# One layer's second group of feed-forward down products issued inside the next layer's attention

## The chip, the cores and the metric

The kernel runs on one core of a Trainium2 chip. The core has five engines that each work through their own queue in order: TensorE (PE, matrix products; its weight loads are listed apart as PEld), VectorE (DVE), ScalarE (ACT), GpSimd (POOL) and SyncE (SP), which here only issues DMA transfers. Matrix products go from SBUF into banks of PSUM, and DVE or ACT carry them out again. The metric is the device time of one execution in microseconds (us): 835.17 us, the median of three runs (834.82 to 837.08).

## The reference, cut to what matters

The input `x` has 4 x 256 tokens of 256 features; a small context has 4 x 64 rows of 64 features. Four layers follow each other. Each one adds a gated cross-attention and then a gated feed-forward block, both on the layer-normalised stream:

```
x = x + tanh(g_xattn[n]) * xattn_n(layernorm(x), ctx)
x = x + tanh(g_ffn[n])   * ffn_n(layernorm(x))
```

The change stands where the feed-forward block of layer 1 meets the attention of layer 2. Layer 1's block has ternary weights:

```
w1_q, w2_q = absmean_quant(w1), absmean_quant(w2)
h   = gelu(layernorm(x) @ w1_q.T + b1)      # 256 -> 1024
out = h @ w2_q.T + b2                       # 1024 -> 256, the "down" product
```

Layer 2's attention has 16 heads of 16 features and a causal mask over 64 keys:

```
qp   = layernorm(x) @ Wq.T
k, v = split(ctx @ Wkv_expand.T)
attn = softmax(where(causal, qh @ kh.T / 4, lowest))
out  = (attn @ vh) @ Wout.T
```

Every token is normalised on its own, so the attention of a token needs that token's row of `x` and the context, and no other token's row.

## The kernel before, in words

The stream `x` stays in SBUF as eight tiles of 128 tokens (NT = 8). They form two groups of four tiles (NG = 2, TPG = 4): tiles 0 to 3 are the first group, tiles 4 to 7 the second.

**How the order is made.** The Python code emits instructions in program order. A planner then makes the queue of every engine before anything runs: the place in program order is an instruction's priority, and where the planner expects an engine to wait, it lets a later instruction that is ready go first. Once made, the queues are fixed, and on the chip an engine waits at the head of its queue. Tiles with a common tag share a fixed number of buffers: products of one bank (`mm`, line 107) have four PSUM banks, and the tag `xn` has seven SBUF buffers, shared by normalised tiles, by `y` of the down products and by `ctxTok`.

**Layer 1's feed-forward, `ffn1` (line 1852).** `up(g)` makes the hidden values of a group: products with the ternary weights (line 1888), Gelu on ACT (line 1895), and a split of the fp32 values into three bf16 terms (lines 1814 to 1817), which are kept in the array `big`. `down(g, terms)` makes the four output tiles of a group: 8 x 3 = 24 bf16 products accumulate in one bank (line 1904), DVE adds the bias into `y` (line 1912), and `gated_add` (line 511) adds the gated result to `x[t]` on DVE. `in_turn` orders this as `up(0), up(1), down(0), down(1)`. Then `used("L1_w1")` and `used("L1_w2")` free two weight buffers and so issue the next weight loads on SP (line 231), and `load_experts3(4, 8)` issues eight transfers on SP (line 330) that overwrite the hidden values with expert weights of layer 3.

**Layer 2's attention, `keyed(2, ...)`.** It first makes keys and values from the context in `keys_values(2, ...)`: products at lines 989 and 1004, eight DVE operations that spread the keys (line 996), and eight copies of values that alternate between ACT and DVE (lines 169 and 171). This needs no row of `x`. Then `attention23` runs `queries(0)`: the normalisation of the first group (statistics at lines 430 and 433, a square root on ACT at line 435, a reciprocal at 438, the normalised tiles at 449), transposes on PE (line 461), the query products (line 476), and a scaling on ACT (line 1033). `in_flight` then walks through the eight tiles as a software pipeline. At step `i` it calls the generator `beside` once, then emits `scores(i)` (score products at line 1057, mask products at 1047; a row maximum at 1070 and two subtractions at 1072 on DVE; an exponential on ACT at 1081), the weights of tile `i-1` (a sum at 490 and a reciprocal at 491 on DVE, a multiplication on POOL at 492), and `attend(i-2)` (transposes at 506, ACT copies at 507, products with the values at 1089, an ACT copy at 1098, the output products at 1101), with the `gated_add` of tile `i-3` at line 511. `beside` holds two streams side by side: `queries(1)`, which is the same three-step chain for the second group, and the keys and values of layer 3 (lines 989, 992, 1004, 1011).

So the second group's normalisation follows `down(1)`, which is complete before anything of layer 2 is emitted.

Of the kernel before, what the change touches and what calls it, by code (L numbers as in the profile page):

```python
# [30 lines left out]
F32 = mybir.dt.float32  # L31
# [5 lines left out]
ALU = mybir.AluOpType  # L37
# [60 lines left out]
def tile_flamingo(ctx: ExitStack, tc: tile.TileContext, a: dict, out: bass.AP):  # L98
# [16 lines left out]
    def region(tag, cols, name):  # L115
        return sb.tile([P, cols], F32, tag=tag, name=name, bufs=1)
# [899 lines left out]
    def attention23(layer, gate, beside):  # L1016
        kbd, vbd = kept.pop(layer)
        w = loaded[f"L{layer}"]
        w_q = w[:, :512].rearrange("p (c o) -> p c o", c=2)
        w_o = w[:, 512:1024].rearrange("p (c o) -> p c o", c=2)  # L1020
        qT = []

        def queries(g):

            xn = layernorm(g, layer == 3)
            yield
            xT = transposed(xn)
            yield
            pss = [ps_mm() for _ in range(2)]
            for half, ps in enumerate(pss):  # L1030
                mm2(ps, lambda c: w_q[:, c, half * P : (half + 1) * P], xT)
            for half, ps in enumerate(pss):
                nc.scalar.mul(xT[:, half, :], ps, 0.25)
            qT.append(xT)

        for _ in queries(0):
            pass

        def scores(t):


            g, i = divmod(t, TPG)
            ps = ps_wide()
            masked = t % 2 == 0
            if masked:
                for a in range(2):
                    nc.tensor.matmul(
                        ps[:, a, :].rearrange("p (h l) -> p h l", l=L),
                        ident16,
                        causal16.unsqueeze(1).to_broadcast([P, 8, L]),  # L1050
                        start=True,
                        stop=False,
                    )

            def part(half, a):
                rows = slice(a * L, (a + 1) * L)
                return nc.tensor.matmul(
                    ps[:, a, half * D : (half + 1) * D],
                    qT[g][rows, half, i * P : (i + 1) * P],
                    kbd[rows, half, t // 2].rearrange("p i l -> p (i l)"),  # L1060
                    start=not masked,
                    stop=(half == 1 or not masked),
                )

            side_by_side(lambda half=half, a=a: part(half, a) for half in range(2) for a in range(2))

            e = t4([P, NH, L], "attn")
            src = ps.rearrange("p a (h l) -> p (a h) l", l=L)
            mx = small([P, NH], "mx")
            nc.vector.tensor_reduce(mx, src, AX.X, ALU.max)  # L1070
            for a in range(2):
                nc.vector.tensor_tensor(
                    e.rearrange("p (f a i) l -> p a f i l", f=2, a=2)[:, a],
                    ps[:, a, :].rearrange("p (f i l) -> p f i l", f=2, l=L),
                    mx[:, a * 8 : (a + 1) * 8]
                    .rearrange("p (f i) -> p f i", f=2)
                    .unsqueeze(3)
                    .to_broadcast([P, 2, 4, L]),
                    ALU.subtract,
                )  # L1080
            nc.scalar.activation(e, e, AF.Exp)
            return e

        def attend(t, e):
            aT = transposed_pairs(e)
            ps = ps_mm()
            for pr in range(NP):
                half, r = divmod(pr, 4)
                nc.tensor.matmul(
                    ps[r * 32 : (r + 1) * 32, half * P : (half + 1) * P],  # L1090
                    vbd[:, t // 2, pr].rearrange("p j d -> p (j d)"),
                    aT[:, pr, :],
                    start=True,
                    stop=True,
                    tile_position=(0, r * 32),
                )
            cT = sb.tile([P, 2 * P], F32, tag="xn", name="ctxTok", bufs=AHEAD + 2)
            nc.scalar.copy(cT, ps[:, : 2 * P])
            ps = ps_mm()
            for half in range(2):  # L1100
                nc.tensor.matmul(
                    ps[:, :D], cT[:, half * P : (half + 1) * P], w_o[:, half, :], start=(half == 0), stop=(half == 1)
                )
            return ps

        in_flight(scores, attend, gate, zip_longest(queries(1), beside))
        if layer == 3:
            used("L3")

# [7 lines left out]
    def keyed(layer, gate):  # L1117
        beside = iter(())
        if layer == 2:
            values = region("wqk", 2048, "values")  # L1120
            for _ in keys_values(2, region("weff", 2048, "kbd2"), values[:, :1024]):
                pass
            beside = beside2(keys_values(3, region("wvo", 2048, "kbd3"), values[:, 1024:]))
        attention23(layer, gate, beside)
        for _ in beside:
            pass
# [725 lines left out]
    def ffn1(gate):  # L1852
        b2_1 = sb.tile([P, 512], F32, tag="low", name="b2_1", bufs=1)[:, :D]
        nc.sync.dma_start(out=b2_1, in_=a["L1_b2"].partition_broadcast(P))
        w1 = ternary(1).rearrange("p (c f) -> p c f", c=2)
        w2 = ternary(2).rearrange("p (f o) -> p f o", f=8)
        hidden = big[:, HIDDEN:].bitcast(BF16).rearrange("p (g k f t) -> p g k f t", g=NG, k=3, f=8)

        def inputs(g):

            two = sb.tile([P, 2, 2, TH], BF16, tag="xT", name="xT", bufs=2)
            more = t4([P, 1024], "more")
            third = more[:, :512].bitcast(BF16).rearrange("p (c t) -> p c t", c=2)
            xn = layernorm(g)
            for c in range(2):
                ps = ps_mm()
                for i, n in enumerate(xn):
                    nc.tensor.transpose(ps[:, i * P : (i + 1) * P], n[:, c * P : (c + 1) * P], ident)
                rest = more[:, 512:]
                nc.scalar.copy(two[:, 0, c, :], ps)  # L1870
                nc.vector.tensor_tensor(rest, ps, two[:, 0, c, :], ALU.subtract)
                nc.scalar.copy(two[:, 1, c, :], rest)
                nc.vector.tensor_tensor(third[:, c, :], rest, two[:, 1, c, :], ALU.subtract)
            return two[:, 0], two[:, 1], third

        xT = [inputs(0)]

        def up(g):
            for f2 in range(4):
                if g == 0 and f2 == 1:  # L1880
                    xT.append(inputs(1))
                h = t4([P, 2, TH], "h")
                for j in range(2):
                    f = 2 * f2 + j
                    ps = ps_mm()
                    for k, term in enumerate(xT[g]):
                        for c in range(2):
                            nc.tensor.matmul(
                                ps,
                                w1[:, c, f * P : (f + 1) * P],  # L1890
                                term[:, c, :],
                                start=(k == 0 and c == 0),
                                stop=(k == 2 and c == 1),
                            )
                    nc.scalar.activation(h[:, j, :], ps, AF.Gelu, bias=b1_1[:, f : f + 1])
                three_terms([hidden[:, g, k, 2 * f2 : 2 * f2 + 2, :] for k in range(3)], h, h, f2 % 2 == 1)
            return hidden[:, g]

        def down(g, terms):
            for i in range(TPG):  # L1900
                ps = ps_mm()
                for f in range(8):
                    for k in range(3):
                        nc.tensor.matmul(
                            ps[:, :D],
                            terms[:, k, f, i * P : (i + 1) * P],
                            w2[:, f, :],
                            start=(f == 0 and k == 0),
                            stop=(f == 7 and k == 2),
                        )  # L1910
                y = sb.tile([P, D], F32, tag="xn", name="y", bufs=AHEAD + 2)
                nc.vector.tensor_tensor(y, ps[:, :D], b2_1, ALU.add)
                gated_add(g * TPG + i, y, gate)

        in_turn(NG, up, down)
        used("L1_w1")
        used("L1_w2")
        load_experts3(EARLY3, E3)


    def quantised():
# [239 lines left out]
```

## Time and profile before

| | |
|---|---|
| median of three runs | 835.17 us |
| the profiled execution | 835.11 us, its span 833.3 us |
| down products of both groups (line 1904) | 192 products, from 510.64 to 531.69 us of the span |
| layer 2 until the first row maximum (line 1070) | 531.69 to 545.73 us |
| first to last score products (line 1057) | 544.23 to 573.33 us |
| last `gated_add` of layer 2's attention (line 511) | ends at 592.95 us |
| busy over the span | PE 93%, DVE 60%, ACT 35%, POOL 30% |

Times in the trace count from the start of the span. A line of the profile's list of instructions in order of time reads: start, duration, engine, line, operation, output <- input, and in brackets how long the engine had been idle and what released it. Products on PE overlap and their ends are modelled, so the step from one start to the next tells more than a single product's duration. PEclk is the clock that the throttle granted to PE, as a share of full speed.

### The profile page before, as it was taken

To read this page: it belongs to the slowest core of one execution; us is meant where nothing else is said; L and a number is where in the kernel's file an instruction comes from. 1 tells how busy PE (TensorE), PEld (TensorE's weight loads), DVE (VectorE), ACT (ScalarE), POOL (GpSimd) and SP (SyncE) were. 2 spreads that over 40 slices of the span, in tenths; PEclk is the share of its full clock that TensorE was granted. 3 is DMA by queue.
4 is the path that set the end of the run, shared out by engine and by line. 5 is a ranking of instruction groups with operands and counts; after the bars stand their busy time and mean duration, and the time that the engine had idled before them with its cause. 6 is when DMAs were issued, how large, how long until landed. Compare 5 with 4: busy or idle time off the path is not lost. (4 is left out here: it accounts for less than half of the span.)

```text
span 833.3 us, 12472 instructions
## 1 busy us (share of the span) xinstructions
PE 773.2 (93%) x4492; PEld 518.9 (62%) x4492; DVE 497.5 (60%) x1146; ACT 291.4 (35%) x508; POOL 246.0 (30%) x211
## 2 busy tenths in 40 slices
PE   6999999898999999999999989998588899999994
PEld 4544433687574777676565746655335556999993
DVE  5565454874682555444869559779769663333331
ACT  2121112343312333232633477166454521233320
POOL 1355454322122343321031300024413203344322
PEclk9999999999999999999999999899879999999998
DMA  9510205700121254324900001810000102232211
GB/s 333 200 39 0 59 37 197 270 20 6 30 69 43 73 140 84 65 45 121 365 33 7 1 1 32 313 42 1 26 1 1 45 9 81 56 46 46 28 17 17
DMA packets 32467, 62.44 MB, mean 75 GB/s; under 512 B 5552, under 2 KB 19504, under 8 KB 31696
## 3 DMA queue, kind: packets, MB, share of 16 engines
q1 hardware_dynamic: 25008, 51.91, 18.2%
q0 software_dynamic: 7104, 9.41, 6.9%
q8 instruction: 39, 0.64, 0.3%
q10 hardware_dynamic: 288, 0.26, 0.1%
q14 instruction: 28, 0.23, 0.1%
HBM read 52.81 MB, written 9.27 MB: 74 GB/s over the span
## 5 line engine op out<-in xcount | busy, mean ns | idle before, releaser
L492 POOL TENSOR_TENSOR attn<-attn,sm 128x1024 f32<-128x1024 f32 x32 | 61.1, 1911 | 229.2 <-DVE sm L491 178.9
L476 PE MATMUL wide<-xT,big 128*128 128x512 f32 (+1 forms) x240 | 108.6, 600 | 1.1 <-DVE shared L1661 0.9
L736 DVE TENSOR_TENSOR rope<-wide,big 128x512 f32<-128x512 f32 x96 | 59.6, 683 | 52.0 <-PE wide L476 52.0
L476 PEld LDWEIGHTS wide<-xT,big 128*128 128x128 f32 (+1 forms) x240 | 43.4, 188 | 57.3 <-issue 49.3
L1434 PE MATMUL wide<-blk,still 128*128 128x128 f32 x640 | 74.8, 275 | 0.6 <-DVE blk L1406 0.6
L1434 PEld LDWEIGHTS wide<-blk,still 128*128 128x128 f32 x640 | 73.1, 192 | 0.8 <-issue 0.8
L708 PE MATMUL mm<-vo,attnT 128*128 128x256 f32 x256 | 58.6, 382 | 1.5 <-ACT attnT L507 1.5
L476 PE MATMUL wide<-xT,dense 128*128 128x512 f32 (+1 forms) x120 | 55.1, 598 | 0.0
L708 PEld LDWEIGHTS mm<-vo,attnT 128*128 128x128 f32 x256 | 47.8, 190 | 11.4 <-ACT attnT L507 3.2
L507 ACT COPY attnT<-mm 128x512 f32<-128x512 f32 x64 | 34.3, 586 | 46.2 <-PE mm L506 45.7
L490 DVE TENSOR_REDUCE sm<-attn 128x16 f32<-128x1024 f32 x32 | 38.6, 1208 | 15.2 <-ACT attn L484 13.8
L1396 DVE COPY still<-big 128x1024 f32 x20 | 13.9, 694 | 52.1 <-PE wide L1434 44.5
L1468 POOL DMA_INDIRECT out_dram<-ring,scratch x20 | 31.5, 1577 | 39.5 <-DVE ring L1461 15.8
L1468 POOL DMA_INDIRECT sums<-ring,big x17 | 26.9, 1580 | 48.3 <-ACT ring L1550 18.9
L1452 PE MATMUL mm<-big,hidden 128*128 x160 | 37.8, 380 | 1.4 <-DVE hidden L1445 1.4
L506 PE MATMUL mm<-ident,attn 128*128 128x128 f32 x256 | 33.7, 275 | 5.7 <-POOL attn L492 5.7
L1369 POOL DMA_INDIRECT xs<-xd,scratch x20 | 20.1, 1003 | 62.3 <-PE mm L1403 39.3
L511 DVE SCALAR_TENSOR_TENSOR x<-mm,tg,x 128x256 f32<-128x256 f32 x44 | 20.5, 471 | 29.5 <-PE mm L708 18.2
L506 PEld LDWEIGHTS mm<-ident,attn 128*128 128x128 f32 x256 | 29.1, 141 | 13.3 <-POOL attn L492 8.5
L1444 ACT ACTIVATE hidden<-wide 128x512 f32<-128x512 f32 x20 | 12.0, 598 | 71.2 <-PE wide L1434 66.1
L476 PEld LDWEIGHTS wide<-xT,dense 128*128 128x128 f32 (+1 forms) x120 | 21.5, 185 | 24.4 <-issue 22.1
L790 ACT COPY big<-mm 128x512 f32<-128x512 f32 x16 | 8.6, 589 | 68.0 <-PE mm L778 61.7
(359 smaller groups left out, 1571.7 us busy)
## 6 DMA issues: line engine op xcount, KB each, us to landing
big<-in_L_w_gate_up SPq DMA_DIRECT2D x8, 1024.0 KB, 10.7
big<-in_L_w_down SPq DMA_DIRECT2D x8, 512.0 KB, 10.8
w_L_qk<-in_L_qk SPq DMA_DIRECT2D x4, 896.0 KB, 9.5
big<-in_L_w SPq DMA_DIRECT2D x2, 1480.0 KB, 8.1
big<-in_L_w SPq DMA_DIRECT2D x2, 1110.0 KB, 5.4
big<-in_L_wo SPq DMA_DIRECT2D x1, 2048.0 KB, 15.0
big<-in_L_w SPq DMA_DIRECT2D x2, 1024.0 KB, 5.2
xd<-xn SPq DMA_DIRECT2D x16, 128.0 KB, 1.8
```

Of the source, the lines that this page charges most:

```text
L476: nc.tensor.matmul(ps, w(c), xT[:, c, :], start=(c == 0), stop=(c == 1))
L490: nc.vector.tensor_reduce(sm, e, AX.X, ALU.add)
L492: nc.gpsimd.tensor_tensor(e, e, sm.unsqueeze(2).to_broadcast([P, groups, n]), ALU.mult)
L506: nc.tensor.transpose(ps[:, i * P : (i + 1) * P], ev[:, pr * P : (pr + 1) * P], ident)
L507: nc.scalar.copy(aT[:, half * 4 : half * 4 + 4, :].rearrange("p i t -> p (i t)"), ps)
L511: return nc.vector.scalar_tensor_tensor(x[t], ps, gate, x[t], ALU.mult, ALU.add)
L708: nc.tensor.matmul(ps[:, :D], aT[:, s, :], vo[:, s, :], start=(s == 0), stop=(s == NP - 1))
L736: nc.vector.tensor_tensor(m[:, s, :].rearrange("q (b t) -> q b t", t=S), ps[:, s, :].rearrange("q (b t) -> q b t", t=S), table, ALU.mult,)
L1369: nc.gpsimd.indirect_dma_start(out=xs, out_offset=None, in_=self.xd, in_offset=bass.IndirectOffsetOnAxis(ap=self.gather[:, b : b + 1].bitc ...
L1434: made = nc.tensor.matmul(ps[:, k, f : f + P], w[:, at : at + P], st[:, c * P : (c + 1) * P], start=(c == 0), stop=(c == 1),)
L1452: made = nc.tensor.matmul(ps[:, :D], hT[:, j * P : (j + 1) * P], self.w[:, bass.ds(r + j * D, D)], start=(j == 0), stop=(j == n - 1),)
L1468: nc.gpsimd.indirect_dma_start(out=self.sums[b % len(self.sums)], out_offset=bass.IndirectOffsetOnAxis(ap=self.scatter[:, b : b + 1].bitca ...
```

## The change

`down` now makes a single tile, `down(g, i, terms)`. `ffn1` makes both groups' hidden values and the first group's four down tiles. The second group's four down tiles go into a generator `others`, which is put into `kept` and stops after its first and its third tile. Its first tile is asked for in `keyed` after the keys and values of layer 2 are emitted. The rest is chained in front of `queries(1)`: step 0 of `in_flight` emits its second and third tile ahead of `scores(0)`; step 1 emits the fourth tile, frees `L1_w2`, issues the transfers of the experts' weights, and goes on to the second group's normalisation, ahead of `scores(1)`. The steps of `queries(1)` thereby stand one step later than before (1, 2 and 3 in place of 0, 1 and 2). `used("L1_w1")` stands ahead of the down products. In layer 3 `kept` holds no `others`, and nothing changes there.

```
-        in_flight(scores, attend, gate, zip_longest(queries(1), beside))
+        in_flight(scores, attend, gate, zip_longest(chain(kept.pop("others", ()), queries(1)), beside))
...
             for _ in keys_values(2, region("weff", 2048, "kbd2"), values[:, :1024]):
                 pass
+            next(kept["others"])
             beside = beside2(keys_values(3, region("wvo", 2048, "kbd3"), values[:, 1024:]))
...
-        def down(g, terms):
+        def down(g, i, terms):
+            ps = ps_mm()
+            for f in range(8):
+                for k in range(3):
+                    nc.tensor.matmul(
+                        ps[:, :D],
+                        terms[:, k, f, i * P : (i + 1) * P],
+                        w2[:, f, :],
+                        start=(f == 0 and k == 0),
+                        stop=(f == 7 and k == 2),
+                    )
+            y = sb.tile([P, D], F32, tag="xn", name="y", bufs=AHEAD + 2)
+            nc.vector.tensor_tensor(y, ps[:, :D], b2_1, ALU.add)
+            gated_add(g * TPG + i, y, gate)
+
+        terms = [up(g) for g in range(NG)]
+        used("L1_w1")
+        for i in range(TPG):
+            down(0, i, terms[0])
+
+        def others():
             for i in range(TPG):
...
-        in_turn(NG, up, down)
-        used("L1_w1")
-        used("L1_w2")
-        load_experts3(EARLY3, E3)
+                down(1, i, terms[1])
+                if i in (0, 2):
+                    yield
+            used("L1_w2")
+            load_experts3(EARLY3, E3)
+
+        kept["others"] = others()
```

## The prediction

> **What bounds the kernel now.** I read the page first: its busy shares and its 40 slices.
>
> ```profile
> PE 773.2 (93%) x4492; PEld 518.9 (62%) x4492; DVE 497.5 (60%) x1146; ACT 291.4 (35%) x508; POOL 246.0 (30%) x211
> ...
> PE   6999999898999999999999989998588899999994
> PEclk9999999999999999999999999899879999999998
> DMA  9510205700121254324900001810000102232211
> ```
>
> PE sets the time nearly everywhere, and slice 25 (521 to 542 us) is one of the few with a lowered clock. That is where layer 1 meets layer 2, so I asked for busy time there by stage: first group's down products, second group's, layer 2 up to its first row maximum, its dense part, its tail.
>
> ```profile
> core 0: us, PE busy (x) PEld busy (x) DVE busy (x) ACT busy (x) POOL busy (x), PEclk, DMA share, GB/s
> 510.64:521.17 10.53, 10.53 (x98) 9.44 (x97) 10.46 (x18) 5.80 (x7) 0.00 (x0) 1.00 0.25 66
> 521.17:531.69 10.52, 10.52 (x98) 9.24 (x96) 6.74 (x20) 0.30 (x1) 0.00 (x0) 1.00 0.85 302
> 531.69:545.73 14.04, 12.22 (x38) 6.19 (x38) 8.63 (x26) 3.01 (x8) 0.00 (x0) 0.76 0.82 297
> 545.73:576.08 30.35, 28.86 (x205) 16.89 (x205) 29.26 (x43) 20.05 (x37) 11.69 (x9) 1.00 0.00 1
> 576.08:592.40 16.32, 11.87 (x117) 7.93 (x116) 12.23 (x39) 10.57 (x21) 6.59 (x6) 1.00 0.00 1
> ```
>
> In the third stage PE has 38 products in 14 us at a mean clock of 0.76; no engine is full, so a chain of latencies bounds it. In the fourth PE and DVE are both full (28.86 and 29.26 of 30.35). In the last, four attends follow each other. The list in order of time gives the steps:
>
> ```profile
> 531.69 1.13 PE L989 MATMUL mm<-ctxT,w_L 64*128 64x256 f32 x4
> 536.86 2.29 PE L461 MATMUL mm<-ident,xn 128*128 128x128 f32 x8
> 539.61 4.69 PE L476 MATMUL mm<-xT,w_L 128*128 128x512 f32 x8 [0.46 <-ACT xT L169]
> 545.62 1.10 PE L461 MATMUL mm<-ident,xn 128*128 128x128 f32 x8
> 548.13 3.70 PE L476 MATMUL mm<-xT,w_L 128*128 128x512 f32 x8
> 558.17 1.14 PE L1057 MATMUL wide<-kbd,xT 64*128 64x256 f32 x8
> 587.99 1.04 PE L506 MATMUL mm<-ident,attn 128*128 128x128 f32 x8
> ...
> 545.73 1.23 DVE L1070 TENSOR_REDUCE mx<-wide 128x16 f32<-128x1024 f32 x1 [4.35 <-PE wide L1057]
> ...
> 548.96 1.28 ACT L1081 ACT_TABLE_LOAD   x1
> ```
>
> The reader sees the same transposes and queries twice: with the clock down for the first group (2.29 and 4.69 us), at full clock for the second (1.10 and 3.70). DVE waits 4.35 us for the first scores.
>
> **The change, part by part.** All sums are against the profiled execution: 835.11 us, span 833.3, so 1.8 us lie around the span; it stands 0.06 us below the median.
>
> *Moved on PE:* 96 products. 192 take 531.69 - 510.64 = 21.05 us, 0.110 each: 2.63 per tile, 10.5 for the group. None goes away; the gain can only be idle PE time that they fill. What PE must do in the third stage, at full clock, from start-to-start steps: four L989 in 0.97; eight L1004 at 0.63 a pair (560.30 to 560.93), 2.5; transposes 1.03 (545.62 to 546.64); queries 3.63 (548.13 to 551.76); scores of a tile 1.06 (556.00 to 557.06). Sum 9.2 of 14.04, so 4.8 us can be filled at most.
>
> *The new order:* PE is done with the first group at 521.17. Priority then goes: keys and values, tile 4's down, queries(0), tiles 5 and 6, scores(0). Tile 4 waits for a bank of `mm`, since keys and values ask for six of the four; these come free with DVE's eight L996 (2.74 us), so tile 4 starts near 525.9 and I leave 0.9 us of PE idle. After that a down tile fills every wait of queries(0). But tiles 5 and 6 also stand ahead of scores(0), so PE has to finish three down tiles first: 3.5 + 3 x 2.63 + 1.03 + 3.63 + 1.06 + 0.9 = 18.0 us. The first row maximum comes near 539.3 in place of 545.73, 6.4 earlier.
>
> *What is pushed into the full stage:* on PE, tile 7's down, 2.63: the gain by PE is 6.4 - 2.6 = 3.8. On DVE, what stood ahead of 545.73 and now stands behind: y, gated add and statistics of tile 7 (0.42 + 0.48 + 0.43 + 0.18 = 1.5), about half of tile 6's (0.75), reciprocal and four normalised tiles (0.17 + 1.38). Sum 3.8; the gain by DVE is 6.4 - 3.8 = 2.6. DVE is the later of the two. It is not the last word, since tile 7's weights leave POOL at 583.7 and its attend starts only at 587.99 behind the other attends: 4.3 us of slack for DVE, none for PE's chain of attends. Between 2.6 and 3.8 I take 3.0, nearer to DVE, which has no slack before 576.
>
> *The second group's chain* becomes tight. Tile 7's down ends near 541.8; y, gated add, statistics to 543.5; root with a table load (1.28 + 0.30) to 545.1; reciprocal and four tiles to 546.9; transposes and copy (1.03 + 0.69) to 548.8; queries to 552.5; scaling to 553.2. Before it ended at 553.23 as well, and scores(4) ran only at 558.17. So the cover is 5 us less the gain; about 2 us remain.
>
> *ACT tables:* before, the second group's root (539.45) shared a table with the first group's, and one load (548.96) leads to the exponentials. Now the root probably falls between the first two exponentials: two more loads, 2 x 1.28 = 2.57 us, on an ACT that is busy 20.05 of 30.35. Bounds: nothing, or 2.57 if attends wait on the copies behind them; an exponential needs 1.06, a row maximum and its subtractions on DVE 2.5, so DVE covers most. I charge 0.4. [...]
>
> *Clock:* the loss is 2.29 - 1.10 + 4.69 - 3.70 = 2.2 us and is part of the 4.8; with PE filled it should not appear. The clock was lowered although no idle of PE above 0.73 us is listed in 531 to 536. [...]
>
> *SP and banks:* the sgu load and the transfers of experts 6 and 7 (five DMAs, issued from 530.37 to 533.54) go to about 542; those of experts 4 and 5 need only the first group's terms, and either stay near 520 or go with them. SP's next transfer is at 592.07 and landing takes 11 us at the median, the experts are used after 676: cost nothing. The `w1` release moves nothing, its load went out at 510.83. POOL's queue gets nothing new; its next work is the first tile's weights (553.02), earlier with the tile. An early down tile holds a bank of `mm` for 2.63 us that attends want: between 0 and one such wait, inside the 0.4 and 0.9 above.
>
> Sum: 3.0 - 0.4 = 2.6 us; 835.1 - 2.6 = 832.5. This is just over 0.3% (2.5 us), which is about what a measurement of this kernel can tell from no change.
>
> **The rivals.** *Everything is filled and the tail shortens* (0.13): the planner lets scores(0) go ahead of a down tile, all 4.8 us come out, and up to 1 us of the attends' backlog: 829.3 to 831. For it: the slack of 4.3 us at tile 7. Against: tiles 5 and 6 have the higher priority.
>
> *The gain is eaten* (0.19): fixed queues meet a wait that the planner costed otherwise (an early y add heading DVE while its products are not done, the two table loads ahead of an exponential). Each such wait is 1 to 1.3 us (DVE idled 1.00 before each y add); two or three take the 2.6: 834.5 to 836. For it: both engines are full from 545.73 on, so nothing hides a stall there.
>
> *The second group's chain becomes the bound, slower* (0.22): the chain has nine changes of engine, and every one can stand behind a tile's operation (1.2 us on DVE, 1.06 on ACT, 1.1 on PE). With one and a half in front of each, 9 x 1.6 = 14.4 us, scores(4) comes at 567.6. From there, one tile's latency (some 13 us: before, tile 0 took from 544.23 to 560.4, less table load and the second group's work) and three more at the pitch of L1101 (5.0 us) end at 596 in place of 592.9: 838. It decides once scores(4) comes later than 564.5. Against: these operations have a higher priority than the tiles' after them.
>
> **How the numbers follow.** The likeliest case (0.46) is 832.5, its own range 830.5 to 834.5; it lies on the border, so I give 0.28 of it to faster and 0.18 to within 0.3%. Faster: 0.28 + 0.13, with 0.01 from the eaten gain, 0.42. Same: 0.18 + 0.18 = 0.36. Slower 0.22. The range goes from 829.3 (835.1 - 4.8 - 1.0) to 838.0, the slower rival's price; about 0.15 lies outside, nearly all above.
>
> **What would show it.** Right: L1904 in pieces between L989, L461 and L476 after 521; full clock from 521 to 545; first row maximum near 539; two extra table loads; scores(4) from 553 to 556; attention ended near 590. Wrong: a clock that still falls, a first maximum after 542 (then tile 7 and the second group are too late to win anything), or scores(4) behind 558.

## The result, and the profile after

The changed kernel takes 843.32 us (median of seven runs, 839.01 to 845.98), the kernel before 837.08 us beside it (seven runs, 834.82 to 838.43). The ratio is 1.0072, with a 95% interval of 1.0051 to 1.0092: some 6 us slower. 832.5 us were predicted, with a range up to 838.0.

The profiled execution took 845.72 us, its span 843.9. The queues of all engines are the same as before up to the first down product and again behind layer 2's attention, so only this stretch differs by design. The profiled execution had lost 3.1 us ahead of it (its first down product starts at 513.76, before at 510.64), which is variation from run to run: among the traces below, whose code is the same up to there, it starts anywhere from 509.20 to 514.44. To leave that out, I count from the end of the first group's down products, called zero below: 521.2 us before, 524.3 after.

| from zero, us | before | changed |
|---|---|---|
| first group's transposes (line 461) | 15.7 | 11.4 |
| first row maximum (line 1070) | 24.6 | 25.7 |
| second group's transposes | 24.4 | 33.0 |
| first attend (line 506) | 33.8 | 37.5 |
| second group's query products (line 476) | 27.0 | 42.4 |
| scores(4) (line 1057) | 37.0 | 47.6 |
| end of the last gated add (line 511) | 71.8 | 79.8 |

So 8.0 us were lost inside the stretch in this execution, which took 2.4 us more than the median of its kernel. The slices of the page, PE and its granted clock:

```profile
PE   6999999899999999999999989988588799999994
PEclk9999999999999999999999999799969999999998
```

Here slice 25 is 527 to 548 us and has a mean clock of 0.7, lower than the 0.8 of before. The stage again by stretches (us, PE, PEld, DVE, ACT and POOL busy with their counts, clock, DMA): keys and values; tile 4; the first group's transposes; its queries; tiles 5 and 6 with scores(0) and the start of tile 7.

```profile
524.33:529.72 5.39, 4.08 (x14) 2.22 (x13) 5.19 (x17) 0.78 (x3) 0.00 (x0) 0.79 0.91 347
529.72:534.78 5.06, 5.03 (x25) 3.39 (x24) 0.65 (x3) 1.84 (x3) 0.00 (x0) 0.54 0.68 247
534.78:537.96 3.18, 1.50 (x9) 0.81 (x9) 3.14 (x9) 0.59 (x1) 0.00 (x0) 0.97 0.00 0
537.96:543.07 5.11, 5.11 (x9) 2.18 (x9) 0.16 (x1) 0.60 (x1) 0.00 (x0) 0.69 0.00 0
543.07:550.05 6.98, 6.98 (x63) 5.82 (x62) 2.95 (x9) 1.88 (x2) 0.00 (x0) 1.00 0.02 4
```

The granted clock is lower behind stretches with gaps: keys and values leave PE idle for 1.3 of 5.4 us, and tile 4 then runs at 0.54. PE is busy during tile 4, and the transposes behind it run at 0.97; these leave gaps again, and the queries behind them run at 0.69. The steps on PE in order of time:

```profile
529.72 5.03 PE L1904 MATMUL mm<-w_L_w,big 128*128 128x256 bf16 x24
535.68 0.41 PE L461 MATMUL mm<-ident,xn 128*128 128x128 f32 x2 [0.93 <-DVE xn L449]
536.31 1.09 PE L461 MATMUL mm<-ident,xn 128*128 128x128 f32 x6 [0.22 <-DVE xn L449]
537.96 5.27 PE L476 MATMUL mm<-xT,w_L 128*128 128x512 f32 x8 [0.56 <-ACT xT L169]
543.07 5.40 PE L1904 MATMUL mm<-w_L_w,big 128*128 128x256 bf16 x48
548.40 1.13 PE L1057 MATMUL wide<-kbd,xT 64*128 64x256 f32 x8
549.47 2.79 PE L1904 MATMUL mm<-w_L_w,big 128*128 128x256 bf16 x24
...
557.37 0.44 PE L461 MATMUL mm<-ident,xn 128*128 128x128 f32 x2 [2.01 <-DVE xn L449]
...
561.81 1.10 PE L506 MATMUL mm<-ident,attn 128*128 128x128 f32 x8
563.80 0.91 PE L1089 MATMUL mm<-attnT,values 128*32 128x128 f32 x16 [0.89 <-ACT attnT L507]
...
565.75 1.13 PE L1101 MATMUL mm<-w_L,ctxTok 128*128 128x256 f32 x4 [0.50 <-ACT ctxTok L1098]
566.72 3.60 PE L476 MATMUL mm<-xT,w_L 128*128 128x512 f32 x8
```

Two things are to be seen. The down tiles (line 1904) stand as whole blocks between the stages of the first group: none lies inside a wait of transposes or queries. And the second group's query products start at 566.72, behind the whole first attend (561.81 to 566.7), although DVE's copy of their input ended at 560.71. DVE shows what both cost:

```profile
534.78 0.42 DVE L1912 TENSOR_TENSOR y<-mm,b 128x256 f32<-128x256 f32 x1 [2.89 <-PE mm L1904]
535.13 0.40 DVE L449 TENSOR_SCALAR xn<-x,mv,rstd 128x256 f32<-128x256 f32 x1
...
573.08 1.23 DVE L1070 TENSOR_REDUCE mx<-wide 128x16 f32<-128x1024 f32 x1 [2.63 <-PE wide L1057]
```

Tile 4's bias add heads DVE's queue and waits 2.89 us for the tile that runs at half clock. The first group's normalised tiles, whose reciprocal had been ready since 531.90, stand behind it. Later DVE, full in this part before, waits 2.63 us for scores(4).

I summed PE's loss over half-microsecond steps from zero: (1 - clock) x busy for the clock, and the rest of each step for idling. In the first 25 us the clock cost 2.9 us before and 4.8 after, idling 1.8 and 3.0; from 25 to 45 us the clock cost 0.0 and 1.7, idling 1.4 and 3.5. Together 6.1 before and 13.0 after. PE's work is the same, and the 6.9 us of difference are most of the 8.0. This sum says where PE lost time and not yet why.

### The profile page after: what moved, and what is told of

It is laid out like the page before. It is cut to its first block, busy times and chain, and to the rows that moved or that the text cites. A ratio compares the mean times of both kernels' runs of the same rounds, so it can differ in the third digit from the quotient of the medians.

```text
span 843.9 us, 12473 instructions
## 1 busy us (share of the span) xinstructions
PE 779.9 (92%) x4489; PEld 523.2 (62%) x4492; DVE 496.6 (59%) x1146; ACT 294.5 (35%) x510; POOL 246.3 (29%) x211
## 5 line engine op out<-in xcount | busy, mean ns | idle before, releaser
L708 PEld LDWEIGHTS mm<-vo,attnT 128*128 128x128 f32 x256 | 47.8, 190 | 11.4 <-ACT attnT L507 3.2
L511 DVE SCALAR_TENSOR_TENSOR x<-mm,tg,x 128x256 f32<-128x256 f32 x44 | 20.5, 470 | 30.1 <-PE mm L708 18.2
L476 PEld LDWEIGHTS wide<-xT,dense 128*128 128x128 f32 (+1 forms) x120 | 21.5, 185 | 24.6 <-issue 23.0
L744 POOL TENSOR_TENSOR rotated<-rope 128x512 f32<-128x512 f32 x12 | 15.3, 1274 | 58.9 <-DVE rope L736 58.9
```

Source lines behind the costliest of these rows:

```text
L476: nc.tensor.matmul(ps, w(c), xT[:, c, :], start=(c == 0), stop=(c == 1))
L511: return nc.vector.scalar_tensor_tensor(x[t], ps, gate, x[t], ALU.mult, ALU.add)
L708: nc.tensor.matmul(ps[:, :D], aT[:, s, :], vo[:, s, :], start=(s == 0), stop=(s == NP - 1))
```

## The experiments

My theory after the result had two parts: the first group's chain is held (by tile 4 and by the clock), and the second group's chain is late and out of place. The rivals were the clock alone and ACT's table loads. Times "from zero" count as above, in the profiled execution of each run; its time and ratio are those of the repeated runs.

**Tile 4 behind queries(0).**

```
         for _ in queries(0):
             pass
+        if "others" in kept:
+            next(kept["others"])
...
-            next(kept["others"])
```

> Times are counted from the end of the first group's down products (521.17 us in the trace of before, 524.33 in that of the changed kernel): first row maximum +24.6 before, +25.7 changed; scores(4) +37.0 and +47.6; end of the last gated add of layer 2's attention +71.8 and +79.8. Here only tile 4's down is emitted behind queries(0). Theory 1 (tile 4's bias add stands ahead of the first group's normalised tiles on DVE and holds that group's chain): normalised tiles start near +8 in place of +10.8, the first row maximum comes near +24, and 1 to 2 us of the 6 us of loss come back. Theory 2 (the loss is the second group's chain, above all the query products queued behind the first attend): scores(4) stays behind +46 and less than 1 us comes back. Theory 3 (lowered clock): the first group's transposes and queries run at half clock as before, under 1 us comes back.

842.79 us beside 836.83; ratio 1.0078 (1.0050 to 1.0106). The normalised tiles started at 7.6, as expected, and the transposes at 8.2. But tiles 4 to 6 then stood as one block of 8.0 us between queries and scores(0), and the first row maximum came at 25.0, where 24 was expected. Scores(4) came at 46.6, the end at 78.8 (79.8 in the changed kernel), and the repeated runs show nothing of it (1.0078 against 1.0072). So the bias add in the way is real, but moving it away is worth 1 us at the most: the block that now stands behind the queries delays scores(0).

**The query products ahead of the first attend.**

```
             xT = transposed(xn)
-            yield
+            if g == 0 or layer == 3:
+                yield
             pss = [ps_mm() for _ in range(2)]
```

> The changed kernel, but the second group's transposes and query products are emitted in one step, so that the query products stand ahead of the first attend as they do before the change. Theory 2: the products start within 1.5 us of their copied input instead of 6 us, scores(4) comes near +42 in place of +47.6, and 3 to 5 us of the loss come back (839 to 840 where the changed kernel has 843). Theories 1 and 3: what is lost before the first row maximum stays (+25.7), under 1.5 us comes back.

845.58 us beside 836.83; 1.0118 (1.0088 to 1.0148). The products came at 36.9 and scores(4) at 42.9, as expected, but nothing of the 3 to 5 us came back. The first attend went from 37.5 to 41.4 and the attention ended at 78.9. PE's list of this kernel:

```profile
557.53 1.66 PE L461 MATMUL mm<-ident,xn 128*128 128x128 f32 x8 [2.01 <-DVE xn L449]
559.20 2.08 PE L1058 MATMUL wide<-kbd,xT 64*128 64x256 f32 x8
561.21 4.01 PE L476 MATMUL mm<-xT,w_L 128*128 128x512 f32 x8
565.15 0.70 PE L989 MATMUL mm<-ctxT,w_L 64*128 64x256 f32 x2
565.78 1.09 PE L506 MATMUL mm<-ident,attn 128*128 128x128 f32 x8
```

Now the first attend (line 506) stands behind the queries. With rows that are this late, one of the two has to wait on PE, and the place of the step only chooses which.

**Keys and values, then all four tiles, then queries(0).**

```
-            next(kept["others"])
+            for _ in kept.pop("others"):
+                pass
```

> Keys and values of layer 2 first, then all four down tiles of the second group, then queries(0); the second group's steps stand as they did before the change. Theory 2: as the second group's chain is again where it was, the time is within 2 us of before (833 to 839). Theory 3: the keys' gaps lower the clock, so the first 20 or so of the 96 down products take 0.21 us each in place of 0.11; this costs 2 to 2.5 us, and the keys that are taken out of the stage behind (5 us) win at most 3. If the clock does not matter, first row maximum near +22, and 2 to 3 us faster than before.

839.32 us beside 836.83; 1.0034 (1.0011 to 1.0058). The second group's steps stand as before and more than half of the loss is gone, though not as much as theory 2 expected (within 2 us). What is left agrees with the clock, granted at 0.50 from 525.5 to 532.3: the 96 products took 13.2 us in place of 10.5, and the first row maximum came at 27.0, the end at 75.3. Taking the keys out of the stage behind gained less than that.

**The four tiles woven into keys, values and queries(0).**

```
-        for _ in queries(0):
+        first = queries(0)
+        next(first)
+        for _ in range(2):
+            next(keys, None)
+            next(keys, None)
+            next(tiles, None)
+        for _ in keys:
+            pass
+        for _ in first:
+            next(tiles, None)
+        for _ in tiles:
             pass
...
-            for _ in keys_values(2, region("weff", 2048, "kbd2"), values[:, :1024]):
-                pass
-            next(kept["others"])
+            kept["keys"] = keys_values(2, region("weff", 2048, "kbd2"), values[:, :1024])
+            next(kept["keys"])
```

Here `others` stops after every tile, `tiles` and `keys` are the two generators taken from `kept`, and `in_flight` gets `queries(1)` alone, as before the change.

> The second group's four down tiles are emitted between the steps of keys and values and of queries(0), one by one, the first group's normalised tiles ahead of them, and all four ahead of scores(0); the second group's normalisation and queries stand as they did before the change. If PE is kept busy, the clock stays at 1.00, the first row maximum comes near +20 to +21 (before +24.6), scores(4) by +37, and the time is 3 to 4 us under before (831 to 834). Theory 3: if the gaps of keys and values lower the clock all the same, first row maximum near +23 and within 1.5 us of before. Theory 2: no part of the changed kernel's loss is left, since the second group's chain is not later than before.

835.55 us beside 836.83; 0.9993 (0.9976 to 1.0009), no difference that can be told, where 3 to 4 us under before were expected with the clock up. The loss of the changed kernel is gone. But tile 4 waited 1.26 us for a bank and took 4.43 us, so the clock fell once more (1.6 us of PE's work, before 2.9). The first row maximum came at 22.6, the end at 72.5.

**Tile 4 inside keys and values.**

```
-            for _ in keys_values(2, region("weff", 2048, "kbd2"), values[:, :1024]):
+            keys = keys_values(2, region("weff", 2048, "kbd2"), values[:, :1024])
+            next(keys)
+            next(keys)
+            next(kept["others"])
+            for _ in keys:
                 pass
-            next(kept["others"])
```

> The changed kernel, with tile 4's down emitted inside keys and values (after the keys and the first of four value products) in place of behind them. Times from the end of the first group's down products. Lowered clock theory (the keys' gaps let the clock fall, tile 4 then takes 5.0 us in place of 2.6, the first group's queries 5.3 in place of 3.6): the gaps are filled, tile 4 takes under 3 us, the first group's transposes start near +8.5 in place of +11.4, and 3 to 4 us of the changed kernel's 6 to 7 us of loss come back. Second group's chain theory (the loss is made behind the first row maximum): the first row maximum comes sooner by 3 us, but the attends end as late as before; under 1.5 us come back.

840.98 us beside 835.56; 1.0058 (1.0038 to 1.0079). Tile 4 took 2.79 us and the transposes started at 8.4, as the clock theory had it. But the clock fell to 0.50 later all the same, near 532.8, within a wait of 2.62 us for the normalised tiles, and the queries were as slow as in the changed kernel:

```profile
526.51 2.79 PE L1907 MATMUL mm<-w_L_w,big 128*128 128x256 bf16 x24
533.41 1.97 PE L461 MATMUL mm<-ident,xn 128*128 128x128 f32 x8 [2.62 <-DVE xn L449]
535.84 5.54 PE L476 MATMUL mm<-xT,w_L 128*128 128x512 f32 x8 [0.46 <-ACT xT L169]
```

The first row maximum came at 23.2 (25.7 in the changed kernel) and the attention ended at 77.2 in place of 79.8. So 2.6 us came back in the trace, less than the 3 to 4 expected, and only part of it is the clock: the tile's bias add no longer stands in the way either. The repeated runs don't tell this kernel from the changed one (1.0058 against 1.0072, with intervals that overlap). The larger part of the loss lies behind.

**The three steps of queries(1) one step later, and nothing else.**

```
+            for _ in kept["others"]:
+                pass
+            kept["others"] = (None,)
             for _ in keys_values(2, region("weff", 2048, "kbd2"), values[:, :1024]):
                 pass
-            next(kept["others"])
```

All down products thus stand where they stood before the change.

> The kernel before, where no down tile is moved, but the three steps of queries(1) are emitted one step of the pipeline later, as the change does. Second group's chain theory: if the place of these steps in the queues costs, then scores(4) comes near +42 to +45 (before +37.0) and the time is 2 to 4 us over before. If it is only the lateness of the second group's down products, the planner has its rows ready and this costs under 1 us.

840.64 us beside 835.56; 1.0061 (1.0035 to 1.0086), 5.1 us by the medians, where 2 to 4 were expected. Its PE list, from the second group's transposes on, and DVE's copy of the query products' input:

```profile
547.00 1.10 PE L461 MATMUL mm<-ident,xn 128*128 128x128 f32 x8
...
555.85 1.97 PE L506 MATMUL mm<-ident,attn 128*128 128x128 f32 x8 [3.27 <-POOL attn L492]
...
560.96 3.60 PE L476 MATMUL mm<-xT,w_L 128*128 128x512 f32 x8
...
566.14 1.13 PE L1057 MATMUL wide<-kbd,xT 64*128 64x256 f32 x8
...
549.42 0.68 DVE L171 COPY xT<-mm 128x512 f32<-128x512 f32 x1
```

The rows are early (transposes at 26.1 from zero, before 24.4), but the query products stand behind the first attend, and PE idles 3.27 us in front of that attend with the queries ready to run behind it. Scores(4) comes at 45.2, the end at 77.4: 5.6 us later than before, from the place of the steps alone. (The clock is part of this: it falls to 0.50 near 555.8, at the end of the wait of 3.27 us, and that attend's transposes take 1.97 us, against 1.09 at 565.12 with the clock at 1.00.)

**Without the two additional table loads.**

```
-        made = nc.scalar.activation(rstd, mv[:, :, 1], AF.Sqrt, bias=eps)
...
+        if kept.get("by DVE"):
+            nc.vector.tensor_scalar(rstd, mv[:, :, 1], EPS, None, ALU.add)
+            nc.vector.reciprocal(rstd, rstd)
+        else:
+            made = nc.scalar.activation(rstd, mv[:, :, 1], AF.Sqrt, bias=eps)
...
```

(for the second group in layer 2; elsewhere as it was)

> The changed kernel, where the second group's normalisation in layer 2 leaves out the square root (it divides by the variance plus epsilon), so that ACT keeps the table of the exponentials: the two additional table loads and the change of engine are gone. If the loads are what makes the second group late: its normalised tiles start 1.5 to 2 us sooner and 2 to 4 us of the loss come back. If they are covered: under 1 us.

870.02 us. The whole time can't be compared here: other values reach layer 3, which picks experts by them. Inside the stretch the normalised tiles started at 30.6 in place of 32.6, as expected, and the attention ended at 79.8, as in the changed kernel. The loads delay the second group by 2 us and cost nothing at the end, since its queries wait for the first attend anyway.

**All four tiles between queries(0) and scores(0), the steps unshifted.**

```
         for _ in queries(0):
             pass
+        for _ in kept.pop("others", ()):
+            pass
...
-            next(kept["others"])
```

> The changed kernel, but all four down tiles stand between queries(0) and scores(0), and the steps of queries(1) stand where they stood before the change. So the second group's rows are late (its last down product ends near +26 in place of 0 before), and no step is shifted. If lateness alone costs: the second group's transposes start near +30 to +31 (before +24.4), its query products hold the first attend behind them, the last gated add of the attention ends near +77 to +79 (before +71.8), and the time is 4 to 7 us over before. If only the shift of the steps costs: the end near +72 to +74, under 2 us over before.

845.30 us beside 836.36; 1.0101 (1.0071 to 1.0131). The second group's transposes started at 30.1, and the first attend, behind its queries, at 41.7. The attention ended at 81.7, which is more than the 77 to 79 expected from lateness. Late rows, without a shifted step, thus go with a loss as large as that of the whole change. But here the four tiles also hold up the first group, whose first row maximum comes at 27.8 (24.6 before), so not all of the loss is the second group's lateness.

**Before, with PE kept busy through keys and values.**

```
-            nc.tensor.matmul(
-                ps[:, :D], ctxT[:, b].rearrange("d j l -> d (j l)"), w_kv[:, D : 2 * D], start=True, stop=True
-            )
+            for _ in range(4 if layer == 2 else 1):
+                nc.tensor.matmul(
+                    ps[:, :D], ctxT[:, b].rearrange("d j l -> d (j l)"), w_kv[:, D : 2 * D], start=True, stop=True
+                )
```

> The kernel before, with each of the four value products of layer 2 made four times over into the same bank (24 more passes of PE, 3.7 us at full clock; the result is the same), to keep PE busy through keys and values. Before lost 2.9 us of PE's work to the lowered clock there. If the clock falls because of the gaps in keys and values: the clock stays at 1.00 until the first transposes, these take 1.1 us in place of 2.3 and the queries 3.7 in place of 4.7; with some 2.4 us of added work outside the gaps the time is within 1.5 us of before. If the clock falls for another reason: it falls all the same and the time is 2 to 4 us over before.

836.10 us beside 836.36; 0.9995 (0.9975 to 1.0016).

```profile
532.73 7.07 PE L1005 MATMUL mm<-w_L,ctxT 64*128 64x256 f32 x32
539.73 1.09 PE L461 MATMUL mm<-ident,xn 128*128 128x128 f32 x8
541.06 3.70 PE L476 MATMUL mm<-xT,w_L 128*128 128x512 f32 x8 [0.24 <-ACT xT L169]
```

The clock stayed at 1.00. Transposes and queries took 1.09 and 3.70 us (2.29 and 4.69 before), and products that nobody needs, three quarters of the 7.07 us or 5.3 (3.7 were expected), cost nothing in the end: what they take beyond the gaps, the higher clock gives back. So the gaps here were what lowered the clock: with work in them (over the first 25 us from zero PE idled 0.3 us, before 1.8) it stayed up.

**Woven, with tile 4 where a bank is free (woven2), and with the third tile ahead of the transposes (woven3).** The first replaces the loop over `range(2)` of the woven kernel; the second adds one line.

```
+        next(keys, None)
+        next(tiles, None)
+        next(keys, None)
+        next(keys, None)
+        next(tiles, None)
         for _ in keys:
             pass
+        next(tiles, None)
         for _ in first:
             next(tiles, None)
```

The last added line is woven3's alone.

> As the woven kernel (all four tiles between the steps of keys, values and queries(0), ahead of scores(0)), but tile 4 stands right behind the first value product, where a bank is free. Lowered clock theory: the woven kernel still lost one stretch of half clock (tile 4 took 4.4 us); here tile 4 takes under 3 us, the clock stays at 1.00, the first row maximum comes near +20.5 in place of +22.6 and the time is 1.5 to 2.5 us under the woven kernel's and 2 to 4 under before. Otherwise as the woven kernel, 0 to 1.5 us under before.

834.08 us beside 835.56; 0.9977 (0.9955 to 1.0000). The clock stayed at 1.00, tile 4 took 2.79 us, the first row maximum came at 20.0. But the first exponential came only at 26.0: in DVE's queue the second group's reciprocal and normalised tiles stood between the row maximum and the second subtraction:

```profile
540.95 1.19 DVE L1082 TENSOR_REDUCE mx<-wide 128x16 f32<-128x1024 f32 x1
...
542.78 1.37 DVE L449 TENSOR_SCALAR xn<-x,mv,rstd 128x256 f32<-128x256 f32 x4
544.07 0.68 DVE L1084 TENSOR_TENSOR attn<-wide,mx 128x512 f32<-128x512 f32 x1
```

The end came at 69.9. By the medians this is 1.5 us under before, where 2 to 4 were expected, and not to be told from the woven kernel.

> As woven2, but the third down tile stands ahead of the first group's transposes, and the fourth between transposes and query products, so that the second group's rows are complete 2 to 3 us sooner, about 3 us ahead of scores(0). Lateness theory: the second group's normalisation no longer stands between the first row maximum and the first exponential (20.0 to 26.0 in woven2), the first exponential comes near +24.5 (before +29.1), the attention ends near +67.5 (before +71.8), and the time is 3.5 to 5 us under before. If lateness does not matter there: as woven2, 1 to 2 us under before.

831.44 us beside 836.36; 0.9943 (0.9920 to 0.9965): 0.57% faster than before, about 4.8 us. The PE list of woven3:

```profile
522.97 2.79 PE L1916 MATMUL mm<-w_L_w,big 128*128 128x256 bf16 x24
525.69 1.13 PE L1004 MATMUL mm<-w_L,ctxT 64*128 64x256 f32 x4
526.75 2.79 PE L1916 MATMUL mm<-w_L_w,big 128*128 128x256 bf16 x24
529.47 0.70 PE L1004 MATMUL mm<-w_L,ctxT 64*128 64x256 f32 x2
530.10 2.79 PE L1916 MATMUL mm<-w_L_w,big 128*128 128x256 bf16 x24
532.73 1.04 PE L461 MATMUL mm<-ident,xn 128*128 128x128 f32 x8
533.61 2.78 PE L1916 MATMUL mm<-w_L_w,big 128*128 128x256 bf16 x24
536.23 3.60 PE L476 MATMUL mm<-xT,w_L 128*128 128x512 f32 x8
```

And its stages: to the end of scores(0), the dense part, the tail.

```profile
521.43:541.20 19.77, 19.72 (x135) 14.04 (x133) 15.31 (x46) 4.70 (x10) 0.00 (x0) 1.00 0.65 232
541.20:570.20 29.00, 27.51 (x201) 16.25 (x200) 27.86 (x41) 20.09 (x37) 10.74 (x8) 1.00 0.26 96
570.20:588.40 18.20, 13.73 (x126) 8.87 (x125) 14.12 (x41) 10.59 (x21) 7.56 (x8) 1.00 0.00 1
```

Every step runs at full clock with a down tile in front of it, and PE is busy 19.72 of 19.77 us. The second group's rows are complete before scores(0): its normalised tiles start at 17.2 (32.6 in the changed kernel) and its query products at 22.2, ahead of the first attend at 29.1. The end came at 67.0, 4.8 us sooner than before.

**What follows.** The rows of the second group and the place of its steps give four cases:

| end of the attention from zero, us | steps as before | steps later |
|---|---|---|
| rows early | 71.8 (before), 67.0 (woven3) | 77.4 (steps_later) |
| rows late | 78.9 (q1_sooner), 81.7 (all_behind_q0) | 79.8 (changed), 77.2 (tile4_in_keys) |

Either alone goes with a loss of 5.6 us or more, and together they cost hardly more than one: in each case the second group's queries and the first attend meet on PE, and one of them waits for the other. Late steps alone are the cleaner test, and their price, 5.1 us in the repeated runs, is most of the changed kernel's 6. With late steps, late rows add nothing that shows: the two such traces without a slow tile 4, `steps_later` and `tile4_in_keys`, end at 77.4 and 77.2 (their first row maxima come at 25.0 and 23.2). In `q1_sooner` the transposes and queries are one step, so its steps stand as before only from the queries on. What the first group wins by running sooner (4.6 us at the first row maximum in woven2, 4.8 in woven3) can't pay for that. The clock is the second cause: filling the keys' gaps moved the end by 2.6 us in two traces (tile4_in_keys against the changed kernel, woven2 against woven). In each, the lowered stretches got shorter by 3.4 us, which is 1.7 us of clock; the rest is idle time that went with them. The repeated runs put it about there: one minus the mean granted clock, times the span, averages 19.0 us over the changed kernel's seven runs and 17.3 to 17.8 over the runs of the kernel before beside the experiments. So some 1.2 to 1.7 of the 6 us are the clock's. Table loads are not a cause.

## Why the prediction was wrong

**The bound and the amount to win: right.** 4.8 us of PE's time were said to be the most that can be filled between 531.69 and 545.73. Woven3 fills all of it and wins 4.8 us. The signs of being wrong that it named all came: a clock that fell, a first row maximum after 542 (550.05), scores(4) behind 558 (571.90).

**"After that a down tile fills every wait of queries(0)": wrong, and the first failure.** I took it that ready products would run in every gap. The planner lays tiles down as blocks: tile 4 ahead of the transposes, tiles 5 and 6 behind the query products. Each stage of the first group still has its own wait, so PE idled 3.0 us in the first 25 us, where 0.9 was allowed. The first row maximum came 25.7 us after zero, where the sum says 18.1.

**"With PE filled it should not appear": wrong.** The clock fell to 0.50 in the keys' gaps (at 527.51; 1.3 us of 5.4 idle, no gap above 0.95) and again behind the transposes (at 537.75). Tile 4 took 5.03 us (2.79 in woven2 at full clock), the queries 5.27 (3.70 in before_warm): 3.8 us of the 7.6 by which the first row maximum was missed. The loss of the kernel before, put at 2.2 us from transposes and queries, is 2.9 when all steps are summed.

**Priority read as order, for DVE.** That tile 4's bias add would head DVE's queue ahead of the first group's normalised tiles was listed only under the rival "the gain is eaten", at 1 to 1.3 us; it waited 2.89.

**The second group's chain: a cover that was not there, and the step that made a gain into a loss.** Its last down product was put near 541.8, 20.6 us from zero; it came 27.9 us from zero. And I costed the chain's steps as if each started when its input was ready. The change's own sentence, that these steps stand one step later, was in the description and got no price: it puts the query products behind the first attend, which alone costs 5.6 us in the trace and 5.1 in the repeated runs (`steps_later`).

**The slower rival: right in its stage, its mechanism and size off.** It said that the second group's chain becomes the bound once scores(4) comes later than 564.5 (43.3 from zero); it came at 47.6. But it priced many short waits behind a tile's operation, against one wait of 6.0 us behind a whole attend, and its 838 is 5 us short (3 us, counted from the kernel before beside it). Its chance was 0.22, and the argument against it (a higher priority than the tiles behind) doesn't hold against what is emitted ahead.

**ACT's tables and SP: right.** Two more loads came (1.28 us each, at 29.3 and 35.9 from zero, the operation behind each starting as it ended, at 554.97 and 561.49) and cost nothing that the end shows; the charge was 0.4. The transfers of the experts went out up to 554.05, about 9 us later than forecast from zero, behind the late last tile, and delayed nothing that the trace shows.

## What to carry to other kernels

When work is moved into a stage's gaps, look at how fine the schedule can cut it, and place it by hand between the steps that wait; a block between two stages fills none of their waits. Look also at who waits for the moved work: here late steps alone cost 5.1 us (`steps_later`), more than the 4.8 us that filling the gaps could win, and a placement that kept rows and steps early and filled the gaps won 4.8 us (`woven3`). A step that is emitted one turn later in a software pipeline can have a price of its own, even where its input is ready: here the query products started at 560.96, 10.9 us behind their copied input. Ask what then stands ahead of it in the queue.

## What the runs showed of the hardware

In the changed kernel PE's granted clock fell at 527.51, behind a single idle stretch of 0.95 us, in the woven kernel near 523.0, at the end of one of 1.26 us; in woven2 it stayed at 1.00 behind one of 1.95 us (up to 543.24). Summed over the first 25 us from zero, idle time counted too, the loss of clock was 1.7 us (woven), 3.4 (before, tile4_in_keys) or 5.1 (changed), always near a multiple of 1.7. The granted clock itself shows why. Here is the changed kernel, divided where its clock changes (columns as above):

```profile
524.10:527.51 3.41, 2.46 (x12) 1.70 (x11) 3.34 (x11) 0.52 (x2) 0.00 (x0) 1.00 0.82 287
527.51:534.34 6.83, 6.47 (x26) 3.83 (x26) 2.73 (x10) 2.10 (x4) 0.00 (x0) 0.50 0.83 317
534.34:537.75 3.41, 1.91 (x12) 0.90 (x9) 2.93 (x9) 0.43 (x1) 0.00 (x0) 1.00 0.00 0
537.75:541.17 3.42, 3.21 (x4) 1.51 (x5) 0.37 (x1) 0.16 (x1) 0.00 (x0) 0.50 0.00 0
```

It is 1.00 or 0.50 here. In the ten traces with a fall in the first 70 us from zero, each lowered stretch there lasts 3.4, 6.8 or 10.2 us, once, twice or three times 3.41; half of 3.41 is 1.7. (Of the others, woven2, woven3 and before_warm, none fell there.) The share of busy time alone doesn't say when it fell: in the kernel before it fell behind 3.41 us in which PE was 79% busy (531.40 to 534.81) and stayed at 1.00 behind others with 51% (483.60 to 487.01). What else decides is not shown. In before_warm 24 more products that nobody reads, 5.3 us of PE's time, kept the clock at 1.00 from zero until the first transposes (521.20 to 539.73) and left the time where it was (ratio 0.9995, 0.9975 to 1.0016).
